# The head of a selective scan: one product a group later on GpSimd, half a ReLU on VectorE, two copies behind the sixth decay

## Chip, cores and metric

The kernel runs on one core of a Trainium2 chip, as one program. The metric is the device time of that core in microseconds (us); lower is better. The engines named below are TensorE (PE, matrix products), VectorE (DVE), ScalarE (ACT), GpSimd (POOL) and SyncE (SP), which here only issues DMA transfers. Each engine runs its own instructions strictly in order; semaphores hold an instruction back until what it needs is done.

## What is computed

Four layers run one after the other on an image batch `x` of shape (2, 128, 64, 64): an attention block, a deformable convolution block, a three-step residual convolution block, and four passes of a selective state-space scan over the flattened image. The change lies where the third layer ends and the fourth begins. Cut to that:

```python
# layer 2 (the third): three Euler steps, then a ReLU
for _ in range(N_STEPS):
    t = jax.nn.relu(_conv(x, w1) + b1[None, :, None, None])
    x = x + H_STEP * (_conv(t, w2) + b2[None, :, None, None])
return jax.nn.relu(x)

# layer 3 (the fourth), for each of four directions; d_inner = 256, N = 16 states
xh = jax.nn.silu(xc)                                # u in the kernel
x_dbl = xh @ W_xp.T
dt, Bm, Cm = ...                                    # split of x_dbl
dt = jax.nn.softplus(dt @ W_dt.T + b_dt)
dA  = jnp.exp(dt[..., None] * A)                    # the decays
dBu = dt[..., None] * Bm[:, :, None, :] * xh[..., None]
h = dA_t * h + dBu_t                                # lax.scan over 4096 positions
y = jnp.einsum('lbdn,bln->bld', hs, Cm)
```

The output is `x` plus a linear fusion of the four directions.

## The kernel before

**Blocks, halves, groups.** The scan works through 64 blocks of 512 positions (2 images, 4 directions, 8 blocks each). A block `i` has two halves `hf` of 128 inner channels, and each half has four groups `ng` of four states, so a block has eight groups, counted through as `k = 8 i + 4 hf + ng`. One group is a tile `db` of 128 partitions by 4 x 512, and its four quarters `q` are scanned one by one.

**What a group costs each engine.**

- VectorE: `db_dve` (line 1868) makes dt·u·B from a PSUM tile, for the groups in which `ND` gives it columns; then four scans (line 1909), each 128x512, whose decays lie in PSUM.
- GpSimd: `db_pool` (line 1877) makes the same product for the columns that VectorE doesn't; then `cmul` (line 1920) multiplies the scanned group by C in place.
- ScalarE: four exponentials `expo` (line 1892, "decays"), each into one of three PSUM buffers `da`, two units ahead of the scan; `keep` (line 1914), which saves the last column of a group and must come before `cmul` overwrites it.
- TensorE: the sums over states (`sums`, line 1928) and the projections.

**The way to a half's inputs.** For each half, `sum_parts` (TensorE, line 1816) and `sum_copy` (ScalarE, line 1819) give dt; `spread` (GpSimd, line 1824) multiplies it with u; `spread_store` (SP, line 1829) writes both to DRAM as `dx`; `spread_load` (SP, line 1837) reads them back in eight transfers of 256 KB, rearranged, into the tile `dd4[hf]`. `expo` and the two `db_` functions of groups `4 hf` to `4 hf + 3` of the block read that tile. For the second half of block 0 the tile is named `dd`, and its first readers are the groups from k = 4 on. VectorE asks for it with `db_dve(4)`, which stands behind the second scan of k = 3.

**The projection of the next block.** `xproj` (TensorE) goes into a PSUM buffer of a pool of two; `xproj_copy` (ScalarE, lines 1777 and 1779) copies it out twice; `bc_store` (SP, line 1783) stores one copy. `sum_parts(0, 1)` takes the PSUM buffer that these two copies empty.

**Order.** Both layers stand under a manual schedule: every engine issues in the order in which the Python code calls. The head, for k = 0 and k = 1, is therefore fixed by the loop from line 2076: in each quarter an `expo` two units ahead, a `scan`, and at certain `k` and `q` extra calls; after the four quarters `cmul(k - 1)`, `db_pool(k + 2)`, and what a block further on needs. SP runs ahead of nothing: a store that waits for GpSimd holds back the loads behind it.

**The end of the third layer.** `outputs(2, 1, 1, 1, ...)` (lines 1339 to 1360) makes the last half image in the tile `mid`, from eight PSUM tiles, on VectorE; line 1360 is its last step. Two calls of `relu` write it to the image `xa` with a step of four elements (16 bytes): rows 0 to 15 on ScalarE (line 1435), rows 16 to 31 on GpSimd (line 1437). The memory of the third layer's tiles is reused by the scan's `db` tiles: the tile of group 1 waits until TensorE has read its last input of the convolutions (line 1316), that of group 2 until `mid` has been read by both calls of `relu`.

Of the kernel before, what the change touches and what calls it, by code (L numbers as in the profile page):

```python
# [1195 lines left out]
def layer2(g, I, hold, E):  # L1196
# [8 lines left out]
    nc, tc = g.nc, g.tc  # L1205
# [5 lines left out]
    with ExitStack() as ctx:  # L1211
# [24 lines left out]
        def inner(t):  # L1236
            return t[:, :, :, 0:NQ]
# [87 lines left out]
        def image_rows(b, n):  # L1325
            return interior(g, b, n * RP, RP).rearrange("p r (i c) -> p c r i", c=4)
# [46 lines left out]
        with tc.manual_schedule():  # L1373
# [57 lines left out]
            def relu(eng, b, n, half=None):  # L1431
                rows = slice(0, RP) if half is None else slice(half * RP // 2, (half + 1) * RP // 2)
                dst, src = image_rows(b, n)[:, :, rows], inner(mid[n])[:, :, rows]
                if eng is nc.scalar:
                    eng.activation(dst, src, AF.Relu)
                else:
                    eng.tensor_scalar(dst, src, 0.0, None, ALU.max)
# [53 lines left out]
            E.rest()  # L1491
            outputs(2, 1, 1, 1, m, sp, saved[1])
            relu(nc.scalar, 1, 1, 0)
            relu(nc.gpsimd, 1, 1, 1)
            E.acc = None


def layer3(g, I, out):
# [5 lines left out]
    nc, tc = g.nc, g.tc  # L1504
# [6 lines left out]
    with ExitStack() as ctx:  # L1511
# [149 lines left out]
        def acc():  # L1661
            return E.acc() if E.acc else psm.tile([P, BLK], F32, name="pm3")
# [62 lines left out]
        NBK = len(blocks)  # L1725
# [47 lines left out]
        def xproj_copy(i):  # L1773

            px = S[i].pop("px")
            S[i]["xd"] = ck.tile([72, BLK], F32, name="xd", bufs=1) if i else xd0
            nc.scalar.copy(S[i]["xd"], px[:72, :])
            bc = S[i]["bc"] = bcs[i % 2]
            nc.scalar.copy(bc[0:32], px[0:32, :])
# [33 lines left out]
        def sum_parts(i, hf):  # L1813
            ps = S[i]["dt", hf] = acc()
            for x in range(2):
                nc.tensor.matmul(ps, g.ident, S[i]["dd", hf][:, x, :], start=(x == 0), stop=(x == 1))  # L1816

        def sum_copy(i, hf):
            nc.scalar.copy(S[i]["dd", hf][:, 0, :], S[i].pop(("dt", hf)))

        def spread(i, hf):
            s_ = S[i]
            dd = s_["dd", hf]
            nc.gpsimd.tensor_mul(dd[:, 1, :], dd[:, 0, :], s_["u"][:, hf, :])

        def spread_store(i, hf):

            S[i]["dx", hf] = dr.tile([P, 2, BLK], F32, name="dx")
            nc.sync.dma_start(S[i]["dx", hf], S[i].pop(("dd", hf)))
# [149 lines left out]
        def front_act(i, slot):  # L1979
            if i < NBK:  # L1980
                if slot == 0:
                    xproj_copy(i)
                elif slot == 1:
                    softplus(i, 0)
                elif slot == 2:
                    softplus(i, 1)
                    sum_copy(i, 0)
                elif slot == 3:
                    sum_copy(i, 1)
                    rest_copy(i)  # L1990
                elif slot == 4:
                    zproj_silu(i)
            if i + 1 < NBK and slot == 7:
                conv_silu(i + 1)


        def transfers(i, slot):
            if i < NBK:
                if slot == 1:
                    bc_store(i)  # L2000
                elif slot == 4:
                    spread_store(i, 0)
                elif slot == 5:
                    spread_load(i, 0)
                    spread_store(i, 1)
            if slot == 0 and 0 < i - 1 < NBK or slot == 1 and i == 1:
                spread_load(i - 1, 1)
            for x, ahead in (("b", 4), ("c", 1)):
                j, ng = divmod(8 * (i - 1) + slot + ahead, 8)
                if ng < NNG and 0 < j < NBK:  # L2010
                    copies(j, x, ng)
# [21 lines left out]
        def front_pool(i, slot):  # L2033
            if i < NBK:
                if slot in (3, 4):
                    spread(i, slot - 3)
# [19 lines left out]
        with tc.manual_schedule():  # L2056
            nc.gpsimd.memset(xt[:, :HC], 0.0)
            nc.gpsimd.memset(xt[:, HC + L :], 0.0)
            nc.gpsimd.memset(xn[:, HB + HW, :HC], 0.0)
            units = [(k, q) for k in range(len(groups)) for q in range(4)]  # L2060
            turns = ((1, 5), (2, 5), (3, 5), (3, 6), (4, 5), (4, 6), (5, 5), (5, 6))
            AHEAD = 2

            for ng in range(NNG):
                for x in "bc":
                    if (x, ng) not in early:
                        copies(0, x, ng)
            for k in range(2):
                weights(k)
            db_dve(0)  # L2070
            db_pool(1)
            for u in range(AHEAD):
                expo(*units[u])
            begin(1)
            conv(1, 1)
            for k in range(len(groups) + 7):
                i, slot = divmod(k, 8)
                live = k < len(groups)
                more = k + 1 < len(groups)
                ended = 1 <= k <= len(groups)  # L2080
                transfers(i + 1, slot)
                if k + 2 < len(groups):
                    weights(k + 2)
                norm = next_norm(i)
                for q in range(4):
                    if norm and slot == 3 and q == 1:
                        ln_log(*norm)
                    if q == 0 and ended:
                        keep(k - 1)
                    if q == 3 and more:  # L2090
                        carry(k + 1, 0)
                    if 4 * k + q + AHEAD < len(units):
                        n = units[4 * k + q + AHEAD]
                        expo(*n)
                        if q != 2:
                            carry(*n)
                    if slot == 6 and q == 0 and 1 <= i < NBK:
                        finish(i - 1)
                    if live:
                        scan(k, q)  # L2100
                    if k == 0 and q == 1:
                        conv_silu(1)
                    elif k == 0 and q == 3:
                        sum_parts(0, 1)
                        sum_copy(0, 1)
                        spread(0, 1)
                        spread_store(0, 1)

                    for j, hf in (((k - 6) // 8, 0), ((k - 10) // 8, 1)):
                        if q == 1 and 8 * j + 6 + 4 * hf == k and 0 <= j < NBK:  # L2110
                            gate(j, hf)
                    if q == 1:
                        if more:
                            db_dve(k + 1)
                        if slot == 5 and 0 <= k - 2 < len(groups):
                            sums(k - 2)
                        if slot == 5 and 1 <= i < NBK:
                            project(i - 1)
                        elif slot == 0 and i == NBK:
                            project_image(i - 1)  # L2120
                            project_half(i - 1, 0)
                        elif slot == 2 and i == NBK:
                            project_half(i - 1, 1)
                            finish(i - 1)
                        front_pe(i + 1, slot)
                        if norm and slot == 0:
                            ln_mean(*norm)
                    if q == 2:
                        front_act(i + 1, slot)
                if norm and slot == 0:  # L2130
                    ln_less(*norm)
                if ended:
                    cmul(k - 1)
                if k + 2 < len(groups):
                    db_pool(k + 2)

                front_pool(i + 1, slot)
                if norm:
                    if slot == 1:
                        ln_square(*norm)  # L2140
                    elif slot == 3:
                        ln_root(*norm)
                    elif slot == 5:
                        ln_scale(*norm)
                    elif slot == 6:
                        ln_store(*norm)
                if live:

                    if (i % (4 * NBLK), slot) in turns:
                        turn(blocks[i][0], turns.index((i % (4 * NBLK), slot)))  # L2150

                if slot != 5 and 0 <= k - 2 < len(groups):
                    sums(k - 2)
                if norm and slot == 2:
                    ln_var(*norm)
# [151 lines left out]
```

## Time and profile before

| what | us |
|---|---|
| median of 4 runs | 5366.66 (5364.16 to 5368.23) |
| the profiled execution, its own time | 5369.85 |
| its span in the profile | 5368.1 |
| VectorE, GpSimd, ScalarE, TensorE busy in the span | 4520.2, 3613.4, 4147.1, 4583.5 |
| of the stretch from 2139 us to the end (3229 us, the scan): VectorE, GpSimd busy | 3188.2, 3192.2 |

The scan takes the last 3229 us of the span, and in it VectorE and GpSimd are each busy for nearly 99% of the time. Both groups of the scan are among the costliest of the page: 1725 scans of 1200 ns with a decay and nothing else carried in (line 1909), and 383 products with C of 4542 ns on GpSimd (line 1920). The first 200 us of the scan hold 9.3 us of VectorE's idle time, while a later stretch of the same length holds 1 to 3 us.

Times of single instructions below are in us from the start of the span. In rows of the order of time the columns are start, duration, engine, line, operation, tiles and shapes, the number of merged instructions, and in brackets the idle time of the engine before it with what ended it.

### The profile page before, as it was taken

The numbers are of one execution on the slowest core, as the hardware profiler recorded it, in microseconds if no ns is written. First come the engines' busy times: TensorE is split into PE (matmuls) and PEld (weight loads), VectorE is DVE, ScalarE is ACT, GpSimd is POOL, SyncE is SP. The second block draws the span as 40 slices with busy tenths as digits, with TensorE's granted clock in tenths as the row PEclk, the third lists the DMA queues.
The fourth block names the chain that finished last, engine by engine and source line by source line (L and its number), as shares of the span: only waits on it lengthen the run. The fifth ranks groups of instructions, "written<-read, shape, count | busy, mean of one in ns | idle before, by whom it ended". The sixth has DMA issues, their size and how long they took to land.

```text
span 5368.1 us, 54874 instructions
## 1 busy us (share of the span) xinstructions
PE 4583.5 (85%) x17062; PEld 1701.7 (32%) x17062; DVE 4520.2 (84%) x4274; ACT 4147.1 (77%) x6595; POOL 3613.4 (67%) x1228
## 2 busy tenths in 40 slices
PE   7999999999997999787777778788788777777776
PEld 3444444444453444222222222222222222222221
DVE  7666665572246996999999999999999999999999
ACT  4999999700266114899899898888899899898897
POOL 5222222110000112999999999999999999999999
PEclk9999999999998999888888888888888888888887
DMA  4111110200484001565565565565565565556554
GB/s 167 49 42 34 48 40 24 46 28 16 81 142 86 8 3 35 130 147 132 133 147 138 132 142 139 130 151 140 136 144 136 133 144 140 133 139 144 135 141 110
DMA packets 331883, 556.46 MB, mean 104 GB/s; under 512 B 53552, under 2 KB 113216, under 8 KB 331456
## 3 DMA queue, kind: packets, MB, share of 16 engines
q1 hardware_dynamic: 330432, 552.22, 43.8%
q8 instruction: 135, 2.21, 0.2%
q14 instruction: 164, 1.34, 0.1%
q10 hardware_dynamic: 1152, 0.68, 0.0%
HBM read 462.38 MB, written 90.31 MB: 103 GB/s over the span
## 4 chain that ended last, share of the span: by engine, by line
PE 35%; DVE 33%; DMA 12%; ACT 10%; issue 5%; POOL 3%; SPq 1%; DVEq 0%; POOLq 0%; ACTq 0%
DVE db L1909 20%; DVE db L1868 9%; PE ps L430 9%; PE acc L446 8%; PE m L1316 6%; PE m L721 5%; DMA c<-bx 5%; DMA dd<-dx 4%; ACT da L1892 4%; POOL db L1920 2%; PE acd L1033 2%; DVE gt L1937 1%; PE m L681 1%; DMA hold<-dx 1%; ACT db L1901 1%
## 5 line engine op out<-in xcount | busy, mean ns | idle before, releaser
L1909 DVE TENSOR_TENSOR_SCAN db<-da,db 128x512 f32<-128x512 f32 x1725 | 1981.8, 1200 | 21.9 <-ACT db L1901 15.1
L1920 POOL TENSOR_TENSOR db<-db,c 128x2048 f32<-128x2048 f32 x383 | 1733.2, 4542 | 22.3 <-ACT lead L1914 21.6
L1928 PE MATMUL py<-db,lead 128*32 128x512 f32 x4096 | 650.7, 721 | 399.0 <-POOL db L1920 396.9
L436 ACT ACTIVATE e<-ps 128x1536 f16<-128x1536 f32 (+1 forms) x683 | 919.8, 1627 | 23.2 <-PE ps L430 23.1
L1892 ACT ACTIVATE da<-dd,lead 128x512 f32<-128x512 f32 x1024 | 704.6, 689 | 163.5 <-DVE db L1909 159.5
L1892 ACT ACTIVATE da<-hold,lead 128x512 f32<-128x512 f32 x1024 | 701.2, 685 | 27.8 <-DVE db L1909 23.2
L1901 ACT ACTIVATE db<-da,db,lead 128x1 f32<-128x1 f32 x1469 | 516.6, 352 | 121.8 <-DVE db L1868 64.4
L1920 POOL TENSOR_TENSOR db<-db,u 128x2048 f32<-128x2048 f32 x128 | 581.0, 4539 | 0.0
L430 PE MATMUL ps<-q 128*128 128x512 f16 x2048 | 553.5, 378 | 3.3 <-issue 2.1
L446 PE MATMUL acc<-e,v 128*128 128x512 f16 x2048 | 553.0, 379 | 0.1
L358 POOL TENSOR_TENSOR parts<-parts 32x512 f32<-32x512 f32 x63 | 79.2, 1257 | 655.0 <-DVE parts L357 655.0
L1746 PE MATMUL pm<-hold,lead 128*128 128x512 f32 x1008 | 461.3, 600 | 1.3 <-ACT xa L1961 1.3
L1868 DVE TENSOR_TENSOR db<-pbc,dd 128x2048 f32<-128x2048 f32 x192 | 435.1, 2266 | 3.5 <-DMA dd<-dx 3.5
L1375 POOL MEMSET hold<- 128x256 f32 x1 | 0.6, 551 | 616.3 <-DVE stat L1175 616.3
L1909 DVE TENSOR_TENSOR_SCAN db<-da,lead,db 128x512 f32<-128x512 f32 x323 | 400.9, 1256 | 5.4 <-POOL db L1877 4.6
L352 DVE RECIPROCAL rec<-acc 32x512 f32<-32x512 f32 x63 | 211.6, 3358 | 189.6 <-PE acc L446 189.3
L1868 DVE TENSOR_TENSOR db<-pbc,hold 128x2048 f32<-128x2048 f32 (+1 forms) x192 | 369.2, 1923 | 0.3 <-PE pbc L1847 0.3
L1928 PEld LDWEIGHTS py<-db,lead 128*32 128x32 f32 x4096 | 90.5, 116 | 768.3 <-POOL db L1920 637.5
L1816 PE MATMUL pm<-hold,ident 128*128 128x512 f32 x508 | 329.3, 782 | 2.2 <-ACT hold L1809 1.6
L1316 PE MATMUL m<-hold,u 128*128 128x512 f32 x648 | 283.6, 599 | 27.8 <-DVE hold L1267 27.8
L1877 POOL TENSOR_TENSOR db<-u,hold 128x2048 f32<-128x2048 f32 x64 | 290.5, 4540 | 0.0
L1877 POOL TENSOR_TENSOR db<-b,dd 128x2048 f32<-128x2048 f32 x64 | 290.2, 4535 | 0.0
(404 smaller groups left out, 7223.0 us busy)
## 6 DMA issues: line engine op xcount, KB each, us to landing
hold<-dx SPq DMA_DIRECT2D x512, 256.0 KB, 6.5
dd<-dx SPq DMA_DIRECT2D x512, 256.0 KB, 6.6
dx<-hold SPq DMA_DIRECT2D x128, 512.0 KB, 3.4
c<-bx SPq DMA_DIRECT2D x768, 64.0 KB, 2.6
u<-bx SPq DMA_DIRECT2D x512, 64.0 KB, 3.0
early<-pos SPq DMA_DIRECT2D x104, 256.0 KB, 10.1
piece<-qd SPq DMA_DIRECT2D x128, 128.0 KB, 2.7
b<-bx SPq DMA_DIRECT2D x256, 64.0 KB, 3.1
```

The lines of the kernel that those rows point to most:

```text
L430: nc.tensor.matmul(ps[:, i, :], t[:, 1, kb * P : (kb + 1) * P], t[:, 0, qb * BLK : (qb + 1) * BLK], start=True, stop=True,)
L436: nc.scalar.activation(e[:, :n, :], ps[:, :n, :], AF.Exp, scale=1.0 / UP**2)
L446: nc.tensor.matmul(acc, v3[b][:, kb, h, :], e[:, i, :], start=(kb == 0), stop=(kb == NS - 1))
L1316: nc.tensor.matmul(m, weights[j][:, dy, x, :], v[j][b][:, x, r0 : r0 + RP, :].rearrange("p r i -> p (r i)"), start=(dy == 0), stop=(dy == 2),)
L1746: nc.tensor.matmul(pu, wcs[:, hf, s, :], window(blk, sgn * s), start=(s == 0), stop=(s == 3))
L1868: nc.vector.tensor_tensor(db_tile(k)[:, :, :n], G[k].pop("pb")[:, :n].unsqueeze(1).to_broadcast([P, 4, n]), S[i]["d4", hf][:, 1, :, :n], A ...
L1877: nc.gpsimd.tensor_tensor(db_tile(k)[:, :, n:], S[i]["b", ng][:, n:].unsqueeze(1).to_broadcast([P, 4, BLK - n]), S[i]["d4", hf][:, 1, :, n ...
L1892: nc.scalar.activation(da, S[i]["d4", hf][:, 0, q, :], AF.Exp, scale=am[:, hf, q, ng : ng + 1])
L1901: nc.scalar.activation(b0, a0, AF.Identity, bias=b0, scale=hl[:, hf, ng, q, :])
L1909: nc.vector.tensor_tensor_scan(d1, d0, d1, 0.0 if zero else hl[:, hf, ng, q, :], ALU.mult, ALU.add)
L1920: eng.tensor_mul(v, v, S[i]["c", ng].unsqueeze(1).to_broadcast([P, 4, BLK]))
L1928: nc.tensor.matmul(S[i]["y", hf][32 * q : 32 * q + 32, :], fold, G[k]["db"][:, q, :], start=False, stop=(ng == NNG - 1),)
```

## The change

Four edits, all of which act once, at the head of the scan.

- The last half of the ReLU (rows 16 to 31) goes from GpSimd to VectorE, where it stands between line 1360 and `db_dve(0)`.
- `front_act(1, 0)`, that is `xproj_copy(1)` with its two copies, goes from quarter 2 to quarter 3 of k = 0, behind the sixth decay. `sum_parts(0, 1)` and `sum_copy(0, 1)` stay behind it.
- `spread(0, 1)` and its store go from k = 0 to k = 1. On GpSimd the product then stands behind `db_pool(2)` and `cmul(0)`, where it stood ahead of both. On SP the store then stands behind `bc_store(1)`, where it stood ahead of it.
- `spread_load(0, 1)` goes from slot 1 to slot 2, so that it still stands behind that store.

```diff
@@ layer2
             relu(nc.scalar, 1, 1, 0)
-            relu(nc.gpsimd, 1, 1, 1)
+            relu(nc.vector, 1, 1, 1)
             E.acc = None
@@ transfers
-            if slot == 0 and 0 < i - 1 < NBK or slot == 1 and i == 1:
+            if slot == 0 and 0 < i - 1 < NBK or slot == 2 and i == 1:
                 spread_load(i - 1, 1)
@@ the loop over k and q
                     if k == 0 and q == 1:
                         conv_silu(1)
                     elif k == 0 and q == 3:
-                        sum_parts(0, 1)
-                        sum_copy(0, 1)
-                        spread(0, 1)
-                        spread_store(0, 1)
+                        front_act(1, 0)
...
-                    if q == 2:
+                    if q == 2 and k:
                         front_act(i + 1, slot)
+                    elif q == 3 and k == 0:
+                        sum_parts(0, 1)
+                        sum_copy(0, 1)
...
                 if k + 2 < len(groups):
                     db_pool(k + 2)
 
+                if k == 1:
+                    spread(0, 1)
+                    spread_store(0, 1)
                 front_pool(i + 1, slot)
```

On TensorE, and everywhere past k = 2, the order of instructions is as before.

## The prediction

> **What bounds the kernel now.** I began with the waits of VectorE and GpSimd past 2139 us, then read the head engine by engine in order of time, then the chain of waits. VectorE first:
>
> ```profile
> 2113.28 1.77 DVE L1348 SCALAR_TENSOR_TENSOR t<-t,t 128x512 f32<-128x512 f32 x1
> ...
> 2133.41 0.68 DVE L1348 SCALAR_TENSOR_TENSOR t<-t,t 128x512 f32<-128x512 f32 x1
> ...
> 2136.68 2.29 DVE L1360 TENSOR_TENSOR mid<-mid,hold 128x2048 f32<-128x2048 f32 x1
> 2139.30 2.29 DVE L1868 TENSOR_TENSOR db<-pbc,hold 128x2048 f32<-128x2048 f32 x1 [0.32 <-PE pbc L1847]
> ...
> 2149.51 0.69 DVE L1678 TENSOR_TENSOR xc<-xa,pm 128x512 f32<-128x512 f32 x1 [3.26 <-PE pm L1670]
> ...
> 2169.09 2.29 DVE L1868 TENSOR_TENSOR db<-pbc,dd 128x2048 f32<-128x2048 f32 x1 [3.54 <-DMA dd<-dx]
> ```
>
> The last row is the one that counts: `db_dve(4)` starts at 2169.09, when the second half's eight loads have landed, 3.54 us after VectorE asked for them. The first two rows are the same instruction; I come back to them. GpSimd, SP, ScalarE, and the chain:
>
> ```profile
> 2113.06 1.44 POOL L1824 TENSOR_TENSOR hold<-hold 128x512 f32<-128x512 f32 x1 [24.63 <-ACT hold L1819]
> ...
> 2139.07 3.85 POOL L1437 TENSOR_SCALAR xa<-mid 128x1024 f32<-128x1024 f32 x1 [11.97 <-DVE mid L1360]
> 2142.75 4.58 POOL L1877 TENSOR_TENSOR db<-u,hold 128x2048 f32<-128x2048 f32 x1
> 2152.77 1.27 POOL L1824 TENSOR_TENSOR hold<-hold,hold 128x512 f32<-128x512 f32 x1 [5.45 <-ACT hold L1819]
> 2153.99 2.30 POOL L1877 TENSOR_TENSOR db<-b,hold 128x992 f32<-128x992 f32 x1
> 2156.24 4.53 POOL L1920 TENSOR_TENSOR db<-db,u 128x2048 f32<-128x2048 f32 x1
> ...
> 2174.05 4.51 POOL L1920 TENSOR_TENSOR db<-db,c 128x2048 f32<-128x2048 f32 x1 [3.08 <-ACT lead L1914]
> ```
>
> ```profile
> 2154.06 0.34 SPq L1829 DMA_DIRECT2D dx<-hold  x1
> 2154.44 0.43 SPq L1783 DMA_DIRECT2D bx<-xd  x1
> 2156.97 3.64 SPq L1837 DMA_DIRECT2D dd<-dx  x8
> ```
>
> ```profile
> 2146.36 0.69 ACT L1751 ACTIVATE hold<-pm,vecs 128x512 f32<-128x512 f32 x1 [0.72 <-PE pm L1746]
> ...
> 2152.11 0.59 ACT L1819 COPY hold<-pm 128x512 f32<-128x512 f32 x1 [1.49 <-PE pm L1816]
> 2152.59 0.20 ACT L1914 COPY lead<-db 128x4 f32<-128x4 f32 x1
> ```
>
> ```profile
> 2160.17 8.84 DMA dd<-dx
> ```
>
> So the head's critical path is: `sum_copy` (ends 2152.69), `spread` (2152.77 to 2154.04), store, loads from 2156.97, the last landing 8.84 us after its issue at 2160.17, thus 2169.01, then `db_dve(4)`. The scans of k = 3 stand behind that, so `keep(3)` does too, and GpSimd waits 3.08 us for it (2174.05). From there to 2440 us the waits of GpSimd show none, and VectorE's sum to 3.1 us (1.5 of it for GpSimd). Whatever moves the landing moves the end by as much.
>
> **The change part by part.** The sum is made as a shift of the landing.
>
> *The later product on GpSimd.* Before, `spread` started 0.08 us after `sum_copy`. Now `cmul(0)` stands ahead. It needs `keep(0)`, which on ScalarE stands behind `sum_copy` (2152.59, 0.20, end 2152.79) and starts about 0.07 later. Its 4.53 us overlap the next instruction by some 0.03, so `spread` starts at 2152.79 + 0.07 + 4.50 = 2157.36: **+4.6**. The store and all eight loads follow it; SP has nothing else to do there. The `bx` store now goes ahead and lands long before (2.6 us). The loads take 12.04 from first issue to last landing (2156.97 to 2169.01), and the same kind took 11.94 to 13.39 around here, so I keep 12.04. The next block's `dx` store will be issued while they still land, but transfers issued behind loads landed behind them here (copies of C issued from 2121.00 landed from 2130.76, the last load at 2130.59), so it costs nothing; shared bandwidth would cost at most its own 2.6. VectorE arrives at `db_dve(4)` at about 2170, still early: the wait grows.
>
> *Copies behind the sixth decay.* On ScalarE the sixth decay (0.68, 0.63 in step) goes ahead of the two copies, which empty the PSUM buffer for `sum_parts`: everything from `sum_parts` on, **+0.6**. The decay itself has its buffer by then (third scan, over at 2145.14).
>
> *The ReLU off GpSimd.* GpSimd is rid of 3.85 us ahead of `db_pool(1)`. That wins nothing by itself: `db_pool(1)` ended at 2147.32, its scan began at 2150.12, behind the 3.26 us that VectorE waited for TensorE. The 0.48 us that k = 2 waited for `db_pool(2)` goes, but ends in the wait for the loads. What matters is when `db_pool(1)` now starts. Its tile is free when TensorE's last line 1316 ends (the merged row from 2127.93, 7.99 us, ends 2135.92); its loads landed by 2130.6. So it runs from about 2136.02 to 2140.60, **across line 1360**, which VectorE starts only at 2136.68.
>
> Now the first two rows: line 1348 took 1.77 instead of 0.68 with two SBUF sources while GpSimd multiplied from 2113.06 to 2114.50; it ended 0.55 after GpSimd. Line 1349, the same kind, took 1.75 at 2086.15 instead of 0.68, and ended 0.55 after a GpSimd product. VectorE stands still meanwhile. Line 1360 has two SBUF sources as well. It would end at about 2140.60 + 2.29 - 0.13 = 2142.76 instead of 2138.97: +3.8. (Bounds: +0 if it starts first, +4.6 at the product's whole length.) The scans read decays from PSUM, and at 2142.83 a scan beside GpSimd took its usual 1.20, so nothing later is held up like that.
>
> The Trainium skill, "SBUF — State Buffer", section "SBUF: two separate sides", has it as an exclusive lock: whichever of a GpSimd instruction and a VectorE one with two SBUF inputs starts first keeps the shared port for its whole length. That speaks against freeing GpSimd at this moment. The rows agree; by the rule, with VectorE first, this term would be 0 and the sum +5.3.
>
> *The ReLU on VectorE.* 128x1024 with a 16-byte step in the destination. No row has it. Nearest: line 891, a one-source clamp into a strided destination, 512 elements in 0.51 on average, 0.62 at most, thus 1.02 to 1.25; line 1089, two sources and a strided destination, 1.05 for 512, thus 2.1; the same work on GpSimd 3.85. From below, line 942 (2048 elements without a step, 1.23) gives 0.6. I take 1.1, by the one-source row.
>
> "VectorE: DVE Perf Modes", section "Mode 2×_2P", lets a single-source fp32 instruction in SBUF make two results a cycle. An estimate from it is 1024 / 2 / 0.96 GHz = 0.53 us, the strided row says twice that, and by the page the sum would be half a us less.
>
> `db_dve(0)` then starts at 2142.76 + 1.1 + 0.03 = 2143.89 instead of 2139.30: +4.6, 0.32 of it hidden by the wait for `pbc`. The scans shift alike, and through the decay buffers ScalarE's fourth decay and SiLU. There 0.72 us of waiting for TensorE hide a part: **+3.9** on all that follows, `sum_parts` included.
>
> Sum: 3.9 + 0.6 + 4.6 = **+9.1 us**: landing at 2178.1, span 5377.2, its own time 5369.85 + 9.1 = 5378.95. That execution lies 3.2 above the median; against the median I say 5366.66 + 9.1 = **5375.8**. A measurement here tells some 0.2% (10.7 us, 5355.9 to 5377.4) from no change, so the forecast is "slower, but within it", close to its edge. Its own range is 5374 to 5378 (ReLU 0.6 to 2.1: +8.6 to +10.1, and the 1.5 by which runs differ).
>
> **The rivals.**
>
> - *The ReLU on VectorE is as dear as on GpSimd* (slower for certain). Place: between line 1360 and `db_dve(0)`. At 3.85 us everything shifts 2.75 more: +11.9, **5378.5**. It decides from 2.7 us on (9.1 + 1.6 = 10.7). For it: ScalarE too needs 2.11 for this half, and 1.90 for a plain copy of twice the size. Against it: strided rows on VectorE cost at most 2.1.
> - *No hold-up at line 1360.* GpSimd starts after VectorE, or the two agree. Line 1360 is on time, the ReLU costs +0.8, which the 0.72 nearly hides: 0.1 + 0.6 + 4.6 = +5.3, **5372.0**. Against it: 0.66 us between the two starts.
> - *The loads don't gate.* Then the 3.54 and 0.48 us of VectorE's waits go: -4.0, **5362.6**. For it: GpSimd idled 5.45 us ahead of `spread`, which looks like room. Against it: the load's landing and `db_dve(4)` are 0.08 us apart, and `spread` now stands behind `cmul(0)`.
> - *The edits don't do what they say*: in the changed order of instructions each is where the diff puts it, and nothing past k = 2 differs. I give it nothing. That later blocks settle in another rhythm can't be priced from the head: another 0.03 us in each of 62 blocks would cross the edge.
>
> **How the numbers follow.** Forecast 0.55, dear ReLU 0.22, no hold-up 0.09, loads don't gate 0.04, another rhythm 0.10. Slower by over 0.2%: a fifth of the forecast (0.11), most of the dear ReLU (0.19), the rhythm (0.10): 0.40. Faster by over 0.2%: the head has no 10.7 us to give, 0.03 for what I don't see. Within: 0.57. The range goes from the hold-up's absence less 1.5 of scatter (5370.5) to the dear ReLU plus 2 (5380.5).
>
> **What would show it.** Line 1877's first product at 2136.0 and line 1360 at about 6.1 us long instead of 2.29; line 1437 on VectorE near 1.1; ScalarE's line 1819 at about 2156.6; `spread` (line 1824) at about 2161.9, right behind the first line 1920; `db_dve(4)` at about 2178.2 with some 8 us of waiting for `dd<-dx`; GpSimd's wait ahead of `cmul(3)` longer by the same. If line 1360 keeps 2.29, the second rival holds. If `db_dve(4)` starts before 2172, my path is wrong; if it is at 2178 and the end moved by something else, the later blocks took up or added time.

## The result, and the profile after

The changed kernel takes 5376.19 us (median of 37 runs, 5371.32 to 5382.43), the kernel before 5366.9 us beside it (57 runs, 5361.65 to 5371.38). The ratio is 1.0018, with a 95% interval of 1.0013 to 1.0023: 7.0 to 12.3 us more. One run of e2 below took 7144.63 us, at a mean granted clock of 0.556, and isn't counted in its ratio.

The spans of the two profiled executions don't show this: 5368.1 us before, 5368.2 us after. The profiled execution of the kernel after, at 5370.01 us, was quicker than any of the 37 runs. In the two profiles the scan begins at different moments. Line 1351 starts at 2135.96 us before and at 2127.94 after, 8.02 us sooner, although all code ahead of it is the same. The table by stretches of time shows where most of that comes from. The columns are the stretch and its length, then the busy time and the number of instructions of TensorE, its weight loads, VectorE, ScalarE and GpSimd, the granted clock, the DMA share and the transfer rate. First the kernel before, then after:

```profile
1420.00:1660.00 240.00, 220.55 (x1845) 128.68 (x1842) 112.11 (x154) 141.49 (x176) 0.00 (x0) 0.98 0.85 140
```

```profile
1420.00:1660.00 240.00, 226.85 (x1936) 132.55 (x1933) 115.45 (x159) 146.88 (x183) 0.00 (x0) 0.98 0.86 145
```

This is the second layer's stretch with the heaviest transfers, at 0.85 of the DMA engines' time. In the same 240 us, after did more (1936 matmuls instead of 1845), at 145 GB/s instead of 140. Ahead of the stretch the kernel after lies 0.73 us behind (the same ScalarE instruction of line 924 starts at 1410.72 before and at 1411.45 after); behind it, it is 6.66 us ahead (line 996 on TensorE, 1662.59 and 1655.93), and the rest of the 8.02 us comes between there and line 1351. Over the nine profiles of this study line 1351 starts anywhere from 2127.9 to 2137.6 us. So spans of single executions can't be compared here. What can be compared is the head, counted from the start of line 1351, and the time from there to the end: 3232.1 us before, 3240.3 after, **8.2 us** more.

VectorE in the head of the kernel after, in order of time:

```profile
2127.94 0.69 DVE L1351 TENSOR_TENSOR mid<-t,m 128x512 f32<-128x512 f32 x1 [0.47 <-PE m L1316]
2128.67 5.99 DVE L1360 TENSOR_TENSOR mid<-mid,hold 128x2048 f32<-128x2048 f32 x1
2134.69 1.12 DVE L1437 TENSOR_SCALAR xa<-mid 128x1024 f32<-128x1024 f32 x1
2135.65 2.27 DVE L1868 TENSOR_TENSOR db<-pbc,hold 128x2048 f32<-128x2048 f32 x1
...
2169.58 2.29 DVE L1868 TENSOR_TENSOR db<-pbc,dd 128x2048 f32<-128x2048 f32 x1 [7.93 <-DMA dd<-dx]
```

Line 1360, with the same operands, takes 5.99 us where it took 2.29. The ReLU behind it takes 1.12. The last row, `db_dve(4)`, starts 41.64 us after line 1351, where it started 33.13 before, and has waited 7.93 us instead of 3.54 for the loads. On ScalarE, `sum_copy` starts 20.28 us after line 1351 instead of 16.15, with `keep(0)` behind it:

```profile
2148.22 0.58 ACT L1819 COPY hold<-pm 128x512 f32<-128x512 f32 x1 [2.08 <-PE pm L1816]
2148.70 0.20 ACT L1914 COPY lead<-db 128x4 f32<-128x4 f32 x1
```

GpSimd in the same stretch:

```profile
2127.99 4.51 POOL L1877 TENSOR_TENSOR db<-u,hold 128x2048 f32<-128x2048 f32 x1 [8.92 <-PE m L1316]
...
2148.98 4.51 POOL L1920 TENSOR_TENSOR db<-db,u 128x2048 f32<-128x2048 f32 x1 [9.80 <-ACT lead L1914]
2153.45 1.27 POOL L1824 TENSOR_TENSOR hold<-hold,hold 128x512 f32<-128x512 f32 x1
...
2174.55 4.51 POOL L1920 TENSOR_TENSOR db<-db,c 128x2048 f32<-128x2048 f32 x1 [8.90 <-ACT lead L1914]
```

The first row starts 0.68 us ahead of line 1360 and ends at 2132.50. Line 1360 ends at 2134.66, that is 2.16 later, or its own 2.29 less 0.13. The product with u (line 1824) now stands directly behind `cmul(0)`, after GpSimd has idled 9.80 us in front of that. SP's queue, and the chain that ended last, where it passes through the loads:

```profile
2154.75 0.34 SPq L1829 DMA_DIRECT2D dx<-hold  x1
2157.42 3.64 SPq L1837 DMA_DIRECT2D dd<-dx  x8
```

```profile
2154.75 2.62 DMA dx<-hold
...
2160.63 8.88 DMA dd<-dx
```

The store lands 2.62 us after its issue. The last of the eight loads, issued at 2160.63, lands 8.88 later, and `db_dve(4)` starts 0.07 behind that. The critical path still runs through the loads; all of it has slid.

### The profile page after: what moved, and what is told of

Its sections match the earlier page's. It is cut to its first block, busy times and chain, and to the rows that moved or that the text cites. A ratio compares the mean times of both kernels' runs of the same rounds, so it can differ in the third digit from the quotient of the medians.

```text
span 5368.2 us, 54876 instructions
## 1 busy us (share of the span) xinstructions
PE 4583.6 (85%) x17062; PEld 1701.3 (32%) x17062; DVE 4524.1 (84%) x4275; ACT 4146.0 (77%) x6595; POOL 3608.9 (67%) x1227
## 4 chain that ended last, share of the span: by engine, by line
PE 36%; DVE 33%; DMA 12%; ACT 10%; issue 5%; POOL 3%; SPq 1%; DVEq 0%; ACTq 0%; POOLq 0%
DVE db L1909 21%; DVE db L1868 9%; PE ps L430 9%; PE acc L446 8%; PE m L1316 6%; PE m L721 5%; DMA c<-bx 5%; DMA dd<-dx 4%; ACT da L1892 4%; PE acd L1033 2%; POOL db L1920 2%; DVE gt L1937 1%; DMA hold<-dx 1%; PE m L681 1%; ACT db L1901 1%
```

## The experiments

Each kernel is the one before with the edit shown, unless it says otherwise. The head's numbers stand together here, each counted in us from the start of line 1351 in that kernel's own profile; "rest" is the time from line 1351 to the end.

| kernel | line 1360 lasts | `sum_copy` | product with u | `db_dve(4)` | rest | ratio to before (95%) |
|---|---|---|---|---|---|---|
| before | 2.29 | 16.15 | 16.81 | 33.13 | 3232.1 | |
| after | 5.99 | 20.28 | 25.51 | 41.64 | 3240.3 | 1.0018 (1.0013 to 1.0023) |
| e1, ReLU back | 2.29 | 16.77 | 22.00 | 38.85 | 3237.6 | 1.0009 (1.0000 to 1.0018) |
| e2, ReLU only | 5.99 | 20.34 | 21.00 | 37.06 | 3235.9 | 1.0006 (0.9997 to 1.0015) |
| e3, later product only | 2.29 | 16.16 | 21.40 | 37.38 | 3236.7 | 1.0007 (0.9999 to 1.0016) |
| e4, copies only | 2.29 | 16.77 | 17.43 | 33.64 | 3232.5 | 1.0002 (0.9993 to 1.0011) |
| e5, ReLU, product held | 2.29 | 16.14 | 16.80 | 33.02 | 3231.8 | 0.9998 (0.9990 to 1.0007) |
| e6, sum first | 2.29 | 13.61 | 14.27 | 30.46 | 3229.7 | 0.9996 (0.9986 to 1.0005) |
| e7, e6 with e5 | 2.29 | 13.60 | 14.26 | 30.39 | 3231.1 | 0.9995 (0.9986 to 1.0004) |

Each of e1 to e7 ran 10 to 12 times. The median of before beside them was 5368.07 us (e1, e2, e3, e5) or 5369.33 us (e4, e6, e7). Of the ratios, after's is the only one whose interval lies wholly above 1; e1's touches it. The verdicts on the parts therefore rest on the rows of the traces, of one profiled execution each.

**e1: the changed order without the moved ReLU.** All edits of the change except the first.

```diff
-            relu(nc.vector, 1, 1, 1)
+            relu(nc.gpsimd, 1, 1, 1)
```

(as a change to the kernel after)

> The changed kernel with one edit undone: the last half of the ReLU is on GpSimd again. I measure the head from the start of line 1351, the last step ahead of the change, to the start of db_dve(4): 33.1 us before, 41.6 us after. Theory (hold-up of line 1360 plus the later product): line 1360 is back at 2.29 us, db_dve(0) follows at once, and what is left is the later product (+4.6) and the copies behind the decay (+0.6): head 38.3, time about 5372. Rival (the whole loss is the later product and its queue, and the hold-up is hidden by the wait for the loads): head stays at 41 to 42, time 5376.

Line 1360 is back at 2.29 and `sum_copy` at 16.77, 0.62 later than before. `db_dve(4)` is 5.72 us later than before. That is 0.96 more than e3 and e4 below have together, because the loads took 12.80 us here from the first issue to the last landing, and 11.93 and 11.94 in those two.

**e2: the moved ReLU alone.**

```diff
-            relu(nc.gpsimd, 1, 1, 1)
+            relu(nc.vector, 1, 1, 1)
```

> The kernel before with one edit: the last half of the ReLU on VectorE. Theory: the first product of line 1877 starts on GpSimd as soon as TensorE is done, line 1360 takes 6.0 us instead of 2.29, line 1437 takes 1.1 on VectorE; db_dve(0) is 4.4 later, 0.7 to 0.9 of that is hidden by ScalarE's wait for TensorE, and the head is 33.1 + 3.6 = 36.7, time about 5370.5. Rival (a hold-up on VectorE is hidden, since VectorE waits 3.3 us for line 1678's input anyway): head 33.1 to 33.5, time 5367.

VectorE and GpSimd:

```profile
2133.94 5.99 DVE L1360 TENSOR_TENSOR mid<-mid,hold 128x2048 f32<-128x2048 f32 x1
2139.97 1.13 DVE L1437 TENSOR_SCALAR xa<-mid 128x1024 f32<-128x1024 f32 x1
```

```profile
2133.27 4.51 POOL L1877 TENSOR_TENSOR db<-u,hold 128x2048 f32<-128x2048 f32 x1 [8.91 <-PE m L1316]
```

The hold-up is the same as after, to 0.01 us, with nothing else of the change there. `db_dve(4)` comes 3.93 us later than before. `sum_copy` is 4.19 later here, more than this edit costs in the kernel after. TensorE was slower ahead of it in this execution: the two matmuls of line 1670 took 1.92 us, and 1.02 before and after; the granted clock from 2147 to 2152 us was 0.66 here, and 1.00 in the same place before and after. From the projection's second copy (line 1779) to `sum_copy` it was 2.64 us before and after and 3.29 here, so some 0.65 of the 4.19 is TensorE's.

**e3: the later product with u alone.**

```diff
                         sum_parts(0, 1)
                         sum_copy(0, 1)
-                        spread(0, 1)
-                        spread_store(0, 1)
...
+                if k == 1:
+                    spread(0, 1)
+                    spread_store(0, 1)
```

(with the loads behind the store, as in the change)

> The kernel before with one edit: spread, its store and its loads of the second half one group later; ReLU on GpSimd and copies where they were. Theory: the product starts behind cmul(0), 4.6 us later, and the head is 33.1 + 4.6 = 37.7, time about 5371.5. Rival (GpSimd's idle 5.4 us ahead of the product and the freed queue take it up): head 33 to 35.

GpSimd:

```profile
2150.70 4.52 POOL L1920 TENSOR_TENSOR db<-db,u 128x2048 f32<-128x2048 f32 x1 [3.37 <-ACT lead L1914]
2155.18 1.27 POOL L1824 TENSOR_TENSOR hold<-hold,hold 128x512 f32<-128x512 f32 x1
```

`sum_copy` stands where it stood before (16.16), but the product with u waits for `cmul(0)` and starts 4.59 us later. `db_dve(4)` follows by 4.25 us; the store ahead of the loads landed in 2.61 us instead of 2.83. GpSimd's idle time ahead of `cmul(0)`, 3.37 us here, was of no use to the product: it stands behind the instruction that waits.

**e4: the copies behind the sixth decay, alone.**

```diff
                     elif k == 0 and q == 3:
-                        sum_parts(0, 1)
...
+                        front_act(1, 0)
...
-                    if q == 2:
+                    if q == 2 and k:
                         front_act(i + 1, slot)
+                    elif q == 3 and k == 0:
+                        sum_parts(0, 1)
...
```

(`sum_copy`, `spread` and `spread_store` go along with `sum_parts`)

> The kernel before with one edit: the projection copies of block 1 go behind the sixth decay, and the sum of the parts, its copy, the product with u and the store follow them as they did. My theory: the sum of the parts waits for the second copy, so all from it on comes one decay (0.63 us) later: copy of the sum 16.8 us after the start of line 1351 instead of 16.15, db_dve(4) at 33.7 instead of 33.13, time 5367.5, which no timing tells from 5366.9. Rival: some waiting of TensorE or ScalarE hides it, and db_dve(4) stays at 33.1.

ScalarE:

```profile
2147.84 1.30 ACT L1892 ACTIVATE da<-hold,lead 128x512 f32<-128x512 f32 x2
2149.08 0.57 ACT L1777 COPY xd<-pm 72x512 f32<-72x512 f32 x1
...
2152.20 0.58 ACT L1819 COPY hold<-pm 128x512 f32<-128x512 f32 x1 [2.08 <-PE pm L1816]
```

The two decays (x2) now run one after the other, the copies behind them, and ScalarE waits 2.08 us for the sum of the parts instead of 1.49. That is 0.62 at `sum_copy` and 0.51 at `db_dve(4)`: small, and not hidden.

**e5: the ReLU on VectorE, but GpSimd's product not across line 1360.** One row of 64 elements stays on GpSimd. It needs line 1360's result, so the product behind it can't start before line 1360 has ended.

```diff
-            relu(nc.gpsimd, 1, 1, 1)
+            relu(nc.vector, 1, 1, 1, (RP // 2, RP - 1))
+            relu(nc.gpsimd, 1, 1, 1, (RP - 1, RP))
```

> The kernel before with the last half of the ReLU on VectorE but for its last row of 64 elements per partition, which stays on GpSimd; that row needs line 1360 and so keeps GpSimd's first product behind it. Theory (the loss is two engines at once, not the ReLU's length): line 1360 is back at 2.29 us, line 1437 on VectorE about 1.1, GpSimd's row starts when VectorE's part is over and its product at about 4.5 us after the start of line 1351; db_dve(0) 0.8 later, nearly all hidden: head 33.1 to 33.4, time 5367. Rival (the ReLU on VectorE costs by itself): head 36.7, as with the ReLU alone.

VectorE and GpSimd (the lines lie 2 or 3 further down in this kernel: 1439 is the ReLU, 1880 the product):

```profile
2138.02 2.29 DVE L1360 TENSOR_TENSOR mid<-mid,hold 128x2048 f32<-128x2048 f32 x1
2140.34 1.06 DVE L1439 TENSOR_SCALAR xa<-mid 128x960 f32<-128x960 f32 x1
```

```profile
2140.40 1.17 POOL L1439 TENSOR_SCALAR xa<-mid 128x64 f32<-128x64 f32 x1 [11.97 <-DVE mid L1360]
2141.47 4.55 POOL L1880 TENSOR_TENSOR db<-u,hold 128x2048 f32<-128x2048 f32 x1
```

With 15 of the 16 rows of the ReLU on VectorE, and the product's start behind line 1360, line 1360 takes its 2.29 again and `db_dve(4)` comes 0.11 sooner than before, not 3.93 later. (The product with u starts as before, to 0.01 us; the 0.11 lies in the loads, which took 11.93 us instead of 12.04.) `db_dve(0)` does start 0.60 us later, but most of ScalarE's 0.72 us of waiting for TensorE goes in exchange, and `sum_copy` is on time. So the price of the moved ReLU is the overlap, not the ReLU.

**e6: the sum of the parts ahead of the projection.** If the landing of the loads sets `db_dve(4)`, then what shortens the way to them must win. Here TensorE makes the norm's mean and the sum of the parts before the projection of block 1, and copy and product come a quarter earlier.

```diff
                     if k == 0 and q == 1:
                         conv_silu(1)
+                        ln_mean(*norm)
+                        sum_parts(0, 1)
                     elif k == 0 and q == 3:
-                        sum_parts(0, 1)
-                        sum_copy(0, 1)
-                        spread(0, 1)
-                        spread_store(0, 1)
+                        front_act(1, 0)
...
+                    elif q == 2:
+                        sum_copy(0, 1)
+                        spread(0, 1)
+                        spread_store(0, 1)
```

(`elif q == 2` belongs to `if q == 2 and k:`; the mean isn't made again for k = 0)

> The kernel before with the sum of the second half's parts (and the norm's mean) issued on TensorE ahead of the projection of block 1 instead of behind it, and its copy and the product with u taken one quarter earlier; the projection's copies go behind the sixth decay. The ReLU stays on GpSimd. My theory: the path to db_dve(4) begins at the copy of the sum, which then comes some 2.8 us earlier: product with u at about 14.0 us after the start of line 1351 instead of 16.81, db_dve(4) at about 30.3 instead of 33.13, VectorE's wait for dd near 0.7 instead of 3.54, time 5364, ratio 0.9995. Rival: the norm and the decays come later by what the sums come earlier, and VectorE itself arrives at 33 or later; then no gain.

VectorE and GpSimd:

```profile
2168.10 2.29 DVE L1868 TENSOR_TENSOR db<-pbc,dd 128x2048 f32<-128x2048 f32 x1 [1.23 <-DMA dd<-dx]
```

```profile
2151.91 1.26 POOL L1824 TENSOR_TENSOR hold<-hold,hold 128x512 f32<-128x512 f32 x1 [2.96 <-ACT hold L1819]
```

The product starts 2.54 us sooner than before, `db_dve(4)` 2.67 us sooner, and VectorE's wait for the loads shrinks from 3.54 to 1.23. The rest is 2.4 us shorter than before. The timing can't separate that from no change.

**e7: e6 with the ReLU of e5.**

> The same as the run before it, and in addition the last half ReLU on VectorE except for one row, which stays on GpSimd behind line 1360 (so that GpSimd's first product cannot start across line 1360). My theory: VectorE arrives 0.6 us later than with the ReLU on GpSimd, and GpSimd's second product is earlier, which takes 0.5 us of VectorE's waiting for db_pool(2): db_dve(4) at 30.2 to 30.9, time 5364, the same as the run before it. Rival: where the loads no longer gate, GpSimd's relief counts, and it is 0.5 to 1 us faster than the run before it.

`db_dve(4)` starts at 30.39, 0.07 from e6: the loads still land last (1.18 us of waiting), and freeing GpSimd of 2.65 us of its ReLU wins nothing. Both have medians 2.6 and 2.8 us under the 5369.33 us of before beside them, with intervals that include 1. By the head both beat before; by the time of the whole run neither can be told from before. In e7's profile the rest is only 1.0 us shorter, though `db_dve(4)` comes 2.74 us sooner. The difference arises at the very end: the last eight matmuls of line 1928 and the last two of line 1955 (1931 and 1958 in this kernel) took 1.93 and 2.08 us, where they took 1.07 and 1.12 before, at a granted clock of 0.64 over the last 13 us instead of 0.89.

## Why the prediction held

The forecast was +9.1 us and 5375.8 us. Measured are +8.5 at `db_dve(4)`, +8.2 from line 1351 to the end, and 5376.19 us, 9.3 above the median of before. The mechanism held in every term of the sum; that the median lies within 0.4 us of the forecast is in part luck, since the terms were off by up to 0.4 and single runs spread over 11 us. Term by term:

- *Line 1360 held up.* Forecast +3.8, measured +3.70, the length of the overlap as worked out from the two short rows. The product started 0.05 us after line 1351, as forecast. e2 and e5 show the cause: the ReLU on VectorE (in e5 but for one row), once with the product across line 1360 (5.99) and once without (2.29). The Trainium skill, "SBUF — State Buffer", section "SBUF: two separate sides", says that of a GpSimd instruction and a VectorE one with two SBUF inputs the one that starts first keeps the shared port to its end. The two rows agree with it: the product started 0.68 us ahead, and line 1360 ended a full own length, less 0.13, behind it.
- *The ReLU on VectorE.* Forecast 1.1, measured 1.12. This settles the likeliest rival, the dear ReLU, which would have needed 2.7 us or more. For 1024 results the strided row of line 891 was the right neighbour, and the unstrided one (0.6) was not. The 0.53 us that the prediction also estimated is half of what was measured; the measurement decides.
- *What reaches `sum_parts`.* Forecast +3.9, measured +3.5: `sum_copy` came 4.13 later, of which e4 shows 0.62 to be the copies. `db_dve(0)` was 4.37 later (forecast 4.6; it started 0.96 us after the ReLU did, ahead of the ReLU's recorded end, and not 1.13). As foreseen, the wait for TensorE between the two SiLU instructions disappeared and took up a part: 4.37 less 0.72 is 3.65.
- *The copies behind the sixth decay.* Forecast +0.6; e4 has 0.62, e1 the same.
- *The product with u behind `cmul(0)`.* Forecast +4.6. From `sum_copy` to the product it was 0.66 us before and 5.23 after, thus +4.57; e3 alone has +4.59. This is the largest term. GpSimd does idle 9.80 us around there in the kernel after, but all of it ahead of `cmul(0)`.
- *Store and loads.* Taken as unchanged, and nearly so: issue to landing of the eight was 12.08 us instead of 12.04, and the store landed in 2.62 instead of 2.83, so the sum at `db_dve(4)` is 8.51 and not 8.70. The 0.2 us of the store goes with the `bx` store: in the six profiles in which `bx` is issued right behind it, the `dx` store took 2.82 to 2.84 us, and in the three in which `bx` had gone ahead (after, e1, e3) 2.61 or 2.62. The next `dx` store did go out during the loads and landed only 4.8 us after its issue, where it had taken 2.6. SP held the next eight loads back for it (their first issue came 42.57 us after line 1351 instead of 37.71), but no engine's wait for these loads shows.
- *The end moves with the landing.* It did, to within the scatter. From `db_dve(4)` to the end it was 3199.0 us before and 3198.6 after, and 3198.8 to 3199.3 in e1 to e6, so the 0.3 us between 8.5 and 8.2 says nothing. (e7, with its slow last matmuls, has 3200.7.)

The parts add up at the product with u, ahead of the transfers: e4's 0.62, e3's 4.59 and e2's 4.19 less the 0.65 of its slower TensorE make 8.75, and after has 8.70. At `db_dve(4)` the sum of the three is 8.69 against 8.51, and that it is so close there is in part luck, since e2's slower TensorE and the shorter loads of e2, e3 and e4 nearly cancel.

Of the other rivals, "no hold-up" falls with the 5.99 us row, and "the loads don't gate" with e6: the landing brought forward by some 2.7 us brought `db_dve(4)` forward by 2.67. That later blocks would settle in another rhythm was not seen: past the first 50 us from line 1351, VectorE idles 28.09 us before and 27.92 after, up to its last instruction.

One sign was read wrongly. GpSimd's wait ahead of `cmul(3)` was to grow by as much as the shift, and grew from 3.08 to 8.90, by 5.8. `cmul(3)` itself starts 8.50 later (46.60 instead of 38.10). But GpSimd arrives at it 2.7 us later too, since its own work ahead of it slid behind the late `cmul(0)`. A wait shows the difference between two arrivals, not the delay of one.

## What to carry to other kernels

Idle time on an engine is room only behind the instruction that waits: a critical step moved behind that instruction inherits its wait and its length, as line 1824 did (+4.57 us). Before taking work off an engine, look at what it will start instead and what that will run beside; here the relieved GpSimd went across VectorE's two-source line 1360 and cost 3.70 us, and one row of 64 elements left as a gate took that price away. Where a wait for a transfer is the last to end, shorten the chain that leads to its issue (e6), and leave the engines that arrive early alone (e7).

## What the runs showed of the hardware

- GpSimd's ReLU on 64 elements took 1.17 us in e5. It started 0.06 us after VectorE's one-source ReLU and ended 0.17 us after it. In e7 the same pair took 1.16 us and ended 0.16 after. At the rate of the 1024 elements (3.81 us) 64 would take some 0.24, by an estimate. So a one-source VectorE instruction, too, may hold GpSimd up when both work in SBUF; this was not tried by itself, and what a GpSimd ReLU as short as this takes alone, no row shows.
- The same ReLU on 1024 elements with a 16-byte step in the destination cost 3.81 to 3.85 us on GpSimd, 2.10 to 2.15 on ScalarE and 1.12 or 1.13 on VectorE.
- Eight loads of 256 KB in the same place took from 11.8 us (e2) to 12.8 us (e1) from the first issue to the last landing. That alone moves `db_dve(4)` by 1.0 us, more than the term of the copies (0.6).
